# Two sequences taking turns through the attention rounds of a fused attention and FFN block

## The chip, the core and the metric

The kernel runs on one core of a Trainium2 chip. The metric is the device time of one execution in microseconds (us). Lower is better. Five engines work side by side, each through its own list of instructions in the order in which the program issues them: PE (TensorE, matrix products), DVE (VectorE), ACT (ScalarE), POOL (GpSimd) and SP, which does no arithmetic here and starts DMA transfers. An instruction waits at the head of its engine's list for what it needs, and everything behind it on that engine waits too.

## What is computed

The input x holds 4 sequences of 512 positions and 512 features. An attention block whose heads are mixed by a Fourier transform is followed by a gated FFN; both sit on a residual:

```python
x = x + attn(layernorm(x))            # per sequence
#  q, kv = n @ W_q.T, n @ W_kv.T      (16 heads of 32)
#  qf, kvf = fft(q), fft(kv), each head divided by its norm
#  kvf = cumsum(kvf, over positions)
#  attn = ifft(qf * kvf).real @ W_o.T
x = x + ffn(layernorm(x))
#  gate, up, down weights are rounded to fp8 first
#  ffn = down(silu(gate(n) * gate_scale) * up(n) * up_scale) * down_scale
```

All is float32, and the running sum over positions goes through a whole sequence.

## The kernel before

The positions are cut into 16 chunks of 128: 4 sequences (b) of TC = 4 chunks (c). The list `chunks` (L71) holds them sequence by sequence, and a round works on chunk i of this list.

**Prologue (L539 to L614).** The three attention weights come in from SP's queue. Layer norm's centring and the transform are folded into them: `centred` (L203) sums a row block on ACT (L206) and centres it on DVE (L207), `fold_in` (L209) multiplies by the transform. For products of nearly float32 precision a folded weight is then held in three parts: a high part (`split_c`, ACT, L219), a low part (`split_d`, a difference on DVE, L223, and a scaling on POOL, L224), and their difference (`split_e`, L227). Chunk 0 runs through its products in between.

**Rounds (L632 to L682), i = 1 to 15.** A round takes chunk i in, and carries older chunks further:
- PE: `main_part(i)`, 16 matmuls (L266); `cross_part(i)`, 8 (L278); from round 4 on `project(i-4)`, the output product (L397, 4 matmuls shown as 8 records); `running(i-1)`, the running sum as a product with a triangle (L342) of a high part kh and a low part kl.
- ACT: the fp8 rounding of one or two FFN weight units, `rounded` (L143, L144; two units a round until round 5, then one until round 13); `taken(i)` (L289); `k_high(i-1)` (L328); `x_a(i+2)` (L248); `squared(i)` (L296); `rooted(i)` (L306); then, in some rounds, the mean and deviation of a finished chunk of sequence 0 (`y_mean`, `y_deviation`, L423 to L432); last `carry(i-1)`, which copies the end of the running sum (L348) and starts, on ACT's own queue, a small DMA that moves its last row to row 0 (L349).
- DVE: `norms(i-1)` (L311 to L314), `scaled(i-1, 0)` (L319), `products(i-2)` (L357, L358), `finish(i-5)` (L405), `v_turn(i-4)`, a transposition into the one buffer qvT that `project` reads (L377), `summed(i)` (L292), `x_d(i+1)` (L256), in rounds 7 to 10 `y_turn` and its difference (L672), `reduced(i)` (L300).
- POOL: `scaled(i-1, 1)` (L319), `carried(i-1)`, which adds the end row of the chunk before (L324), `combined(i-2)` (L366, L367), `k_low(i-1)` (L333), `x_b(i+2)` (L252).
- SP: loads of inputs and raw weight units (`load_x`, `load_wanted`), the way of a chunk through memory (`v_out`, `v_back`; for sequence 0 also `y_out`, `y_back`), and stores.

The running sum of a chunk needs the end of the chunk before it. In list order that is the previous round: cum(i-1) at the end of round i gives the row that `carried(i)` adds in round i+1.

**The test of the weights (L146 to L199).** In round 14 `flagged` folds sums of the rounded weights into one flag. At the end of round 15's code POOL clears three scratch tiles (L162 to L164), reads the flag and passes a switch; for ordinary weights it jumps over a long arm that would round the weights again. The FFN's products wait for it, since the arm would write the weights.

**FFN (L684 to L769).** For each sequence 12 steps (n counts all 48): 16 matmuls of gate and up (L480), SiLU and product on ACT and DVE, 8 matmuls down (L518). What is left of attention is dealt out to the first steps: `on_pe(0)` the running sum and products of chunk 15, `on_pe(1..4)` the last four `project`, `behind(1..4)` their `finish`. LATE and the tail after L755 set the order of the last steps.

Of the kernel before, what the change touches and what calls it, by code (L numbers as in the profile page):

```python
# [7 lines left out]
F32 = mybir.dt.float32  # L8
# [12 lines left out]
HK = HD // 2  # L21
EPS = 1e-5


# [11 lines left out]
def tile_fft_attention_then_fp8_ffn(  # L36
# [33 lines left out]

    chunks = [(b, c) for b in range(B) for c in range(TC)]  # L71
    N = len(chunks)

    tab = const.tile([P, 3, P], F32, name="tab")
    nc.scalar.dma_start(tab[:, 0, :], tables[:, 0, :])
# [23 lines left out]
    def load_xT(i):  # L101
        xTs[i] = work.tile([P, KC, P], F32, tag="xT", name=f"xT_{i}")
        nc.sync.dma_start(xTs[i], xT[i])

# [51 lines left out]
    def round_again(ok):  # L156
# [7 lines left out]
        on.tensor_copy(f8, a, saturate=False)  # L164
        index = nc.values_load(
# [36 lines left out]

    def centred(raw, j, i):  # L203
        each = work.tile([P, D], BF16, tag="each", name=f"each_w{i}{j}", bufs=1)
        less = small.tile([P, 1], F32, tag="less", name=f"less_w{i}{j}", bufs=8)
        nc.scalar.activation(each, raw[:, j, :], AF.Copy, accum_out=less)  # L206
        nc.vector.tensor_scalar(raw[:, j, :], raw[:, j, :], float(D), less, ALU.mult, ALU.subtract)  # L207

# [112 lines left out]
    def carried(i, on=None):  # L321
        if i in ends:
            row = kqs[i][:1, 0, :]
            (on or nc.gpsimd).tensor_tensor(row, row, ends.pop(i), ALU.add)  # L324

# [19 lines left out]
    def carry(i):  # L345
        if 0 <= i and chunks[i][1] + 1 < TC:
            end = work.tile([P, D], F32, tag="end", name=f"end_{nm(i)}", bufs=1)
            nc.scalar.copy(end[P - 32 :, :], cums[i][P - 32 :, :])  # L348
            nc.scalar.dma_start(end[:1, :], end[P - 1 :, :])  # L349
            ends[i + 1] = end[:1, :]  # L350

# [65 lines left out]
    def y_tile(b, c):  # L417
        return xt[b * TC + c] if b == 0 else ys[b][:, c, :]

    def y_mean(b, c):  # L420
        less = small.tile([P, 1], F32, tag="less", name=f"less_{b}_{c}", bufs=8)
        each = work.tile([P, D], BF16, tag="each", name=f"each_{b}_{c}", bufs=1)
        nc.scalar.activation(each, y_tile(b, c), AF.Identity, accum_out=less)  # L423
        nc.scalar.activation(less, less, AF.Copy, scale=-1.0 / D)
        st_y[b, c] = less

    def y_deviation(b, c):
        less = st_y[b, c]
        rstd = small.tile([P, 1], F32, tag="dev", name=f"dev_{b}_{c}", bufs=8)
        each = work.tile([P, D], BF16, tag="each", name=f"each_d{b}_{c}", bufs=1)  # L430
        nc.scalar.activation(each, y_tile(b, c), AF.Square, bias=less, accum_out=rstd)
        nc.scalar.activation(rstd, rstd, AF.Identity, scale=1.0 / D, bias=eps)  # L432
        nc.gpsimd.tensor_tensor(rstd, rstd, nhalf, ALU.pow)  # L433
        st_y[b, c] = less, rstd

    def y_norm(b, c):
        less, rstd = st_y.pop((b, c))
        xn = work.tile([P, D], F32, tag="xn", name=f"xn_{b}_{c}")
        nc.vector.tensor_scalar(xn, y_tile(b, c), less, rstd, ALU.add, ALU.mult)
        xns["y", b, c] = xn  # L440
        if b == 0:
            del xt[c]

# [108 lines left out]
    for j in range(KC):  # L552
        load_raw(raw_o[j // 2][:, j % 2, :], w_oT, j)
    load_xT(2)
    nc.sync.dma_start(gus[:, 0, :], gate_scale)
# [8 lines left out]
    idle = ps.tile([P, 2, D], F32, tag="tp", name="idle", bufs=1)  # L564
    for n in range(8):
# [6 lines left out]
    for j in range(KC):  # L572
        centred(raw_kv, j, 0)
        for i in range(KC):
            fold_in(pk[i], raw_kv, i, j)
    pq = [ps.tile([P, D], F32, tag="b", name=f"pwq{i}") for i in range(2)]
    t = ps.tile([P, 2, D], F32, tag="tp", name="pwq", bufs=1)
    pq += [t[:, i, :] for i in range(2)]
    for j in range(KC):
        centred(raw_q, j, 1)  # L580
        for i in range(KC):
            fold_in(pq[i], raw_q, i, j)
        if j == 1:
            x_a(0)
            x_b(0)
        split_c(wkv, pk[j], j)
        split_d(wkv, pk[j], j, "kv")
    x_d(0)
    x_a(1)
    x_b(1)  # L590
    main_part(0, 0)
    for i in range(KC):
        split_c(wq, pq[i], i)
        split_d(wq, pq[i], i, "q")
        split_e(wkv, i, nc.vector)
        if i == 1:
            for j in range(2):
                fold_out(raw_o[0][:, j, :], j)
    main_part(0, 1)
    for i in range(KC):  # L600
        split_e(wq, i, (nc.vector, nc.gpsimd)[i % 2])
    taken(0)
    nc.vector.tensor_copy(tri_r, tri)
    cross_part(0)
    x_a(2)
    x_b(2)
    summed(0)
    x_d(1)
    load_xT(3)
    squared(0)  # L610
    reduced(0)
    for j in range(2):
        fold_out(raw_o[1][:, j, :], 2 + j)
    rooted(0)  # L614

# [12 lines left out]
    def load_wanted():  # L628
        while wanted:
            load_unit(wanted.pop(0))  # L630

    for i in range(1, N):  # L632
        at(load_x, i - 4)
        at(v_back, i - 3)
        c = i - 2 - 5
        if 0 <= c < TC:
            y_back(0, c)
# [12 lines left out]
        k_low(i - 1)  # L650
        at(finish, i - 5)
        at(v_turn, i - 4)
        at(x_a, i + 2)
        at(x_b, i + 2)
        at(v_out, i - 2)
        c = i - 1 - 5
        if 0 <= c < TC:
            y_norm(0, c)
            y_out(0, c)
        load_wanted()  # L660
        if i == N - 2:
            ok = flagged()
        if i == N - 1:
            round_again(ok)
        cross_part(i)
        summed(i)
        at(x_d, i + 1)
        at(load_xT, i + 3)
        squared(i)
        c = i - 2 - 5  # L670
        if 0 <= c < TC:
# [7 lines left out]
        if 0 <= c < TC:  # L679
# [11 lines left out]
    scaled(N - 1, 0, nc.vector)  # L691
    scaled(N - 1, 1, nc.gpsimd)
    carried(N - 1)
    combined(N - 2)
    v_back(N - 3)
    load_x(N - 4)
    v_out(N - 2)
    nc.sync.dma_start(dsc, down_scale.partition_broadcast(P))
    k_high(N - 1)
    k_low(N - 1)  # L700
    v_turn(N - 4)
    load_y(0)
    load_x(N - 3)
    v_back(N - 2)
    load_y(1)

    def on_pe(n):
        if n == 0:
            running(N - 1, "tp")
            products(N - 1)  # L710
            combined(N - 1)
            v_out(N - 1)
            v_turn(N - 3)
        elif n <= 4:
            project(N - 5 + n, "tp")

# [5 lines left out]
    def behind(n):  # L722
        b, m = divmod(n, MC)
        if 1 <= n <= 4:
            finish(N - 5 + n)
            if n == 1:
                load_x(N - 2)
                v_back(N - 1)
                v_turn(N - 2)
            elif n == 2:  # L730
                load_x(N - 1)
                v_turn(N - 1)
# [98 lines left out]
```

## Time and profile before

| | us |
|---|---|
| median of 3 runs | 480.39 (479.73 to 483.82) |
| the profiled execution, its time | 482.49 |
| its span, first to last instruction | 480.7 |
| TensorE busy | 445.1, 93% of the span |
| VectorE busy | 242.7, 50% |
| ScalarE busy | 215.7, 45% |
| GpSimd busy | 156.6, 33% |
| mean granted TensorE clock | 0.974 |

The profile page gives busy time per engine, the span in 40 slices, and the costliest groups of instructions. A row of a timeline gives the start, the duration, engine, source line and operation, tile written and tiles read, and in brackets how long the engine was idle before and what ended the idle time. In the text "round r starts at" means the start of its first L266 matmul: 28.8 for round 1, 39.75, 50.35, 60.1, 71.5, 81.4, 95.0, 106.5, 119.35, 130.4, 141.5, 152.6, 162.1, 171.4 and 181.1 for round 15, whose last matmul ends at 190.7.

### The profile page before, as it was taken

What the parts mean: (1) busy time and instruction counts of PE and PEld (TensorE: products, weight loads), DVE (VectorE), ACT (ScalarE), POOL (GpSimd) and SP (SyncE); (2) the same over time, 40 slices, a digit from 0 to 9 for tenths busy, and PEclk for the clock granted to TensorE, in tenths of its full rate; (3) what the DMA queues carried; (4) which work ended last, traced back from release to release, by engine and by line L of the source; (5) the groups of instructions that cost most, each with busy time, mean ns of one, the idle gap of its engine ahead of it and who ended that gap; (6) DMA issues with size and microseconds to landing.
All of it is one profiled execution on the core that took longest, in us unless ns stands there. A gap on an engine that the chain in (4) does not pass through costs nothing.

```text
span 480.7 us, 5386 instructions
## 1 busy us (share of the span) xinstructions
PE 445.1 (93%) x1810; PEld 337.3 (70%) x1810; DVE 242.7 (50%) x373; ACT 215.7 (45%) x386; POOL 156.6 (33%) x153
## 2 busy tenths in 40 slices
PE   8787789888888998599999999999999999999996
PEld 7455556455555665476688888888888888888885
DVE  3866476658888787422433343333352343522235
ACT  6448687767657633211353323543325533222230
POOL 1745765556457756400001231112140022400000
PEclk9998799899999999799999999999999999999999
DMA  8133768577976542493133004141050430100002
GB/s 305 41 109 110 191 173 258 150 201 197 248 204 172 158 109 81 95 262 92 41 89 84 6 35 142 44 105 27 1 175 10 102 65 1 65 24 0 0 1 87
DMA packets 91615, 51.21 MB, mean 107 GB/s; under 512 B 70592, under 2 KB 71104, under 8 KB 91584
## 3 DMA queue, kind: packets, MB, share of 16 engines
q1 hardware_dynamic: 90912, 50.62, 38.1%
q8 instruction: 14, 0.23, 0.2%
q10 hardware_dynamic: 672, 0.22, 0.2%
q14 instruction: 17, 0.14, 0.1%
HBM read 34.03 MB, written 16.78 MB: 106 GB/s over the span
## 4 chain that ended last, share of the span: by engine, by line
PE 57%; issue 1%; POOL 1%; DVE 0%; ACT 0%; POOLq 0%; another core or an unknown queue 0%; DVEq 0%
PE gu L480 36%; PE pd L518 18%; PE po L397 3%; DVE o L529 0%; POOL kl L333 0%; POOL kq L324 0%; POOL kq L319 0%; DVE o L530 0%; PE cum L342 0%; ACT gf L490 0%; ACT kh L328 0%; POOLq L172 0%; POOLq L827 0%; DVEq L529 0%
## 5 line engine op out<-in xcount | busy, mean ns | idle before, releaser
L491 DVE SCALAR_TENSOR_TENSOR gf<-gu,gus,gf 128x512 f32<-128x512 f32 x48 | 35.9, 748 | 124.1 <-PE gu L480 118.3
L480 PE MATMUL gu<-yh,wg 128*128 128x512 f32 x192 | 75.9, 395 | 2.5 <-DVE nt L312 2.5
L518 PE MATMUL pd<-wd,fh 128*128 128x512 f32 (+1 forms) x204 | 77.7, 384 | 0.0
L480 PE MATMUL gu<-yl,wg 128*128 128x512 f32 x192 | 75.8, 395 | 0.0
L518 PE MATMUL pd<-wd,fl 128*128 128x512 f32 (+1 forms) x204 | 75.8, 377 | 0.0
L480 PE MATMUL gu<-yh,wu 128*128 128x512 f32 x192 | 74.7, 389 | 0.0
L480 PE MATMUL gu<-yl,wu 128*128 128x512 f32 x192 | 74.7, 389 | 0.0
L499 ACT CAST fh<-gf 128x512 fp32r<-128x512 f32 x48 | 29.8, 620 | 94.4 <-DVE gf L491 94.4
L397 PE MATMUL po<-wo,qvT 128*128 128x512 f32 x128 | 59.9, 612 | 8.7 <-DVE qvT L377 8.7
L490 ACT ACTIVATE gf<-gu,gus 128x512 f32<-128x512 f32 x48 | 33.1, 689 | 64.6 <-PE gu L480 64.0
L500 DVE TENSOR_TENSOR fl<-gf,fh 128x512 fp32r<-128x512 f32 x48 | 35.9, 747 | 33.1 <-ACT fh L499 33.1
L397 PEld LDWEIGHTS po<-wo,qvT 128*128 128x128 f32 x128 | 24.2, 194 | 36.5 <-issue 28.0
L433 POOL TENSOR_TENSOR dev<-dev,nhalf 128x1 f32<-128x1 f32 x16 | 8.8, 553 | 109.0 <-ACT dev L432 109.0
L518 PEld LDWEIGHTS pd<-wd,fl 128*128 128x128 f32 x204 | 38.4, 188 | 8.1 <-issue 1.0
L518 PEld LDWEIGHTS pd<-wd,fh 128*128 128x128 f32 x204 | 38.3, 188 | 8.2 <-issue 0.7
L480 PEld LDWEIGHTS gu<-yh,wg 128*128 128x128 f32 x192 | 36.7, 191 | 10.3 <-POOLq L172 2.9
L480 PEld LDWEIGHTS gu<-yl,wg 128*128 128x128 f32 x192 | 36.7, 191 | 7.5
L480 PEld LDWEIGHTS gu<-yh,wu 128*128 128x128 f32 x192 | 36.2, 189 | 7.5
L480 PEld LDWEIGHTS gu<-yl,wu 128*128 128x128 f32 x192 | 36.1, 188 | 7.5
L737 POOL TENSOR_TENSOR yl<-t,yh 128x512 fp32r<-128x512 f32 x12 | 15.5, 1293 | 54.9 <-ACT yh L464 54.9
L319 POOL TENSOR_TENSOR kq<-kq,rn 128x512 f32<-128x512 f32 x16 | 21.7, 1355 | 34.9 <-DVE rn L314 28.9
L292 DVE TENSOR_TENSOR kq<-pp,kq 128x1024 f32<-128x1024 f32 x16 | 19.6, 1225 | 21.4 <-PE pp L278 11.8
(109 smaller groups left out, 716.3 us busy)
## 6 DMA issues: line engine op xcount, KB each, us to landing
xT<-in_xT SPq DMA_DIRECT2D x16, 256.0 KB, 4.0
qv_all<-qv SPq DMA_DIRECT2D x16, 256.0 KB, 2.2
zv<-qv_all SPq DMA_DIRECT2D x64, 64.0 KB, 3.7
x<-in_x SPq DMA_DIRECT2D x16, 256.0 KB, 4.4
y_all<-x SPq DMA_DIRECT2D x16, 256.0 KB, 2.1
xn_all<-xn SPq DMA_DIRECT2D x16, 256.0 KB, 2.3
z<-xn_all SPq DMA_DIRECT2D x64, 64.0 KB, 2.6
ys<-y_all SPq DMA_DIRECT2D x16, 256.0 KB, 4.0
```

The costliest lines, as they stand in the source:

```text
L292: nc.vector.tensor_tensor(kqs[i], sqs.pop(i), kqs[i], ALU.add)
L319: on.tensor_tensor(t, t, r, ALU.mult)
L397: nc.tensor.matmul(po, lhsT=qvT[:, k, :], rhs=wo[:, k, :], start=k == 0, stop=k == KC - 1)
L433: nc.gpsimd.tensor_tensor(rstd, rstd, nhalf, ALU.pow)
L480: nc.tensor.matmul(p, lhsT=w[:, k, m * P : (m + 1) * P], rhs=v[:, k, :], start=k == 0 and v is yhs[b], stop=k == KC - 1 and v is yls[b],)
L490: nc.scalar.activation(g, pgu[0], AF.Silu, scale=gus[:, 0, m : m + 1])
L491: nc.vector.scalar_tensor_tensor(f, pgu[1], gus[:, 1, m : m + 1], g, ALU.mult, ALU.mult)
L499: nc.scalar.copy(fh, f)
L500: nc.vector.tensor_tensor(fl, f, fh.bitcast(F32), ALU.subtract)
L518: nc.tensor.matmul(p, lhsT=v[:, c * P : (c + 1) * P], rhs=wd[:, m, s], start=m == 0 and v is fused[n][0], stop=m == MC - 1 and v is fused[ ...
L737: nc.gpsimd.tensor_tensor(*y_turn(b + 1, m - 7), ALU.subtract)
```

## The change

- The list of chunks alternates between two sequences: (0,0), (1,0), (0,1), (1,1) and so on, then sequences 2 and 3. The end of a chunk is now needed two list places later.
- The end row's DMA goes from ACT's queue to SP's, at the head of the next round (`carry_on`).
- Order inside a round. ACT: `rooted(i-1)` and `carry(i-2)` stand at the head of round i, so `rooted` comes after the mean and deviation. DVE: `reduced` ahead of `y_turn`. POOL: `x_b(i+1)` at the head, `carried` ahead of `scaled(.., 1)`, and the difference of `y_turn`, which leaves DVE. SP: `carry_on`, `v_back`, `y_back`, `load_x`, units. Sequence 0 is finished in rounds 5, 7, 9, 11 (mean and deviation), turned in 7, 9, 11, 13.
- The low part of a folded weight is one DVE operation that reads PSUM; two of the row sums of W_q go to DVE, its centring to POOL.
- The switch is moved up in round 15, ahead of `combined(13)` and `k_low(14)`, and the three clears are gone.
- The last running sum, the four last `project` and `finish` come one FFN step later, and `scaled(15, 1)` on POOL comes after `k_low(15)`.

The diff, cut to its core:

```diff
-    chunks = [(b, c) for b in range(B) for c in range(TC)]
+    chunks = [(b + d, c) for b in range(0, B, 2) for c in range(TC) for d in range(2)]
+    place = {bc: i for i, bc in enumerate(chunks)}
...
-        on.memset(ab, 0.0)
-        on.memset(cd, 0.0)
-        on.tensor_copy(f8, a, saturate=False)
...
     def split_c(w, pw, i):
-        nc.scalar.activation(w[0][:, i, :], pw, AF.Copy, scale=UNDER)
+        nc.scalar.activation(w[0][:, i, :], pw, AF.Copy, scale=UNDER / SPLIT)
-    def split_d(w, pw, i, name):
-        d = work.tile([P, D], F32, tag="cross", name=f"d_{name}{i}")
-        nc.vector.tensor_tensor(d, pw, w[0][:, i, :].bitcast(F32), ALU.subtract)
-        nc.gpsimd.tensor_scalar(w[1][:, i, :], d, SPLIT, 1.0, ALU.mult, ALU.mult)
+    def split_d(w, pw, i):
+        nc.vector.scalar_tensor_tensor(
+            w[1][:, i, :], w[0][:, i, :].bitcast(F32), -SPLIT, pw, ALU.mult, ALU.add
+        )
...
     def carry(i):
-        if 0 <= i and chunks[i][1] + 1 < TC:
-            end = work.tile([P, D], F32, tag="end", name=f"end_{nm(i)}", bufs=1)
+        b, c = chunks[i]
+        if c + 1 < TC:
+            end = work.tile([P, D], F32, tag="end", name=f"end_{nm(i)}")
             nc.scalar.copy(end[P - 32 :, :], cums[i][P - 32 :, :])
-            nc.scalar.dma_start(end[:1, :], end[P - 1 :, :])
-            ends[i + 1] = end[:1, :]
+            ends[i] = end
+    def carry_on(i):
+        if i in ends:
+            end = ends.pop(i)
+            nc.sync.dma_start(end[:1, :], end[P - 1 :, :])
+            b, c = chunks[i]
+            ends[place[b, c + 1], "row"] = end[:1, :]
...
-    for j in range(KC):
-        centred(raw_q, j, 1)
+    def fold_q(j, on_act):
+        centred(raw_q, j, row_sum(raw_q, j, 1, on_act), nc.gpsimd)
         for i in range(KC):
             fold_in(pq[i], raw_q, i, j)
...
     for i in range(1, N):
+        rooted(i - 1)
+        at(carry, i - 2)
+        at(carry_on, i - 2)
+        at(v_back, i - 3)
+        if (c := y_due(i, 2)) is not None:
+            y_back(0, c)
         at(load_x, i - 4)
-        at(v_back, i - 3)
...
         load_wanted()
         norms(i - 1)
         scaled(i - 1, 0, nc.vector)
+        at(x_b, i + 1)
+        carried(i - 1)
         scaled(i - 1, 1, nc.gpsimd)
         at(products, i - 2)
-        carried(i - 1)
+        if i == N - 2:
+            ok = flagged()
+        if i == N - 1:
+            round_again(ok)
         at(combined, i - 2)
...
         squared(i)
-        c = i - 2 - 5
-        if 0 <= c < TC:
-            nc.vector.tensor_tensor(*y_turn(0, c), ALU.subtract)
         reduced(i)
+        if (c := y_due(i, 2)) is not None:
+            nc.gpsimd.tensor_tensor(*y_turn(0, c), ALU.subtract)
+        rounded(i, 1)
+        if (c := y_due(i, 0)) is not None:
+            y_mean(0, c)
+            y_deviation(0, c)
         at(project, i - 4)
         running(i - 1)
-        rounded(i, 1)
-        rooted(i)
-        c = i - 5
-        if 0 <= c < TC:
-            y_mean(0, c)
-            y_deviation(0, c)
-        carry(i - 1)
...
     def on_pe(n):
-        if n == 0:
+        if n == 1:
             running(N - 1, "tp")
...
-        elif n <= 4:
-            project(N - 5 + n, "tp")
+        elif 2 <= n <= 5:
+            project(N - 6 + n, "tp")
```

`y_due(i, late)` gives the chunk of sequence 0 that is due, in every second round: `c, odd = divmod(i - late - 5, 2)`.

More of the change, by code (lines that the diff above doesn't have):

```diff
@@ L199, in round_again, with row_sum, centred @@
                     on.tensor_copy(to[:, k, :], c)
-    def centred(raw, j, i):
-        each = work.tile([P, D], BF16, tag="each", name=f"each_w{i}{j}", bufs=1)
+    def row_sum(raw, j, i, on_act=True):
         less = small.tile([P, 1], F32, tag="less", name=f"less_w{i}{j}", bufs=8)
-        nc.scalar.activation(each, raw[:, j, :], AF.Copy, accum_out=less)
-        nc.vector.tensor_scalar(raw[:, j, :], raw[:, j, :], float(D), less, ALU.mult, ALU.subtract)
+        if on_act:
+            each = work.tile([P, D], BF16, tag="t8", name=f"each_w{i}{j}", bufs=1)
+            nc.scalar.activation(each, raw[:, j, :], AF.Copy, scale=-1.0, accum_out=less)
+        else:
+            nc.vector.tensor_reduce(less, raw[:, j, :], AX.X, ALU.add, negate=True)
+        return less
+    def centred(raw, j, less, on):
+        on.tensor_scalar(raw[:, j, :], raw[:, j, :], float(D), less, ALU.mult, ALU.add)
     def fold_in(pw, r, i, j):
@@ L321, in carried @@
     def carried(i, on=None):
-        if i in ends:
+        if (i, "row") in ends:
             row = kqs[i][:1, 0, :]
-            (on or nc.gpsimd).tensor_tensor(row, row, ends.pop(i), ALU.add)
+            (on or nc.gpsimd).tensor_tensor(row, row, ends.pop((i, "row")), ALU.add)
     def k_high(i):
@@ L417, in y_tile @@
     def y_tile(b, c):
[L418 removed]
+        return xt[place[b, c]] if b == 0 else ys[b][:, c, :]
     def y_mean(b, c):
         less = small.tile([P, 1], F32, tag="less", name=f"less_{b}_{c}", bufs=8)
[L422 removed]
+        each = work.tile([P, D], BF16, tag="t8", name=f"each_{b}_{c}", bufs=1)
         nc.scalar.activation(each, y_tile(b, c), AF.Identity, accum_out=less)
@@ L441, in y_norm @@
         if b == 0:
-            del xt[c]
+            del xt[place[b, c]]
     def y_out(b, c):
@@ L564, in tile_fft_attention_then_fp8_ffn @@
     idle = ps.tile([P, 2, D], F32, tag="tp", name="idle", bufs=1)
-    for n in range(8):
+    for n in range(10):
         nc.tensor.matmul(
@@ L578, in tile_fft_attention_then_fp8_ffn @@
     pq += [t[:, i, :] for i in range(2)]
-    for j in range(KC):
-        centred(raw_q, j, 1)
+    def fold_q(j, on_act):
+        centred(raw_q, j, row_sum(raw_q, j, 1, on_act), nc.gpsimd)
         for i in range(KC):
             fold_in(pq[i], raw_q, i, j)
[L583 to L587, printed above, removed]
+    fold_q(0, True)
+    split_c(wkv, pk[0], 0)
+    fold_q(1, False)
+    split_d(wkv, pk[0], 0)
+    x_a(0)
+    x_b(0)
+    for i in range(1, KC):
+        split_c(wkv, pk[i], i)
+        split_d(wkv, pk[i], i)
+        if i == 1:
+            fold_q(2, True)
+    fold_q(3, False)
+    main_part(0, 0)
+    x_a(1)
+    for i in range(2):
+        split_e(wkv, i, nc.gpsimd)
     x_d(0)
-    x_a(1)
-    x_b(1)
-    main_part(0, 0)
     for i in range(KC):
         split_c(wq, pq[i], i)
-        split_d(wq, pq[i], i, "q")
-        split_e(wkv, i, nc.vector)
+        split_d(wq, pq[i], i)
         if i == 1:
@@ L598, in tile_fft_attention_then_fp8_ffn @@
                 fold_out(raw_o[0][:, j, :], j)
+    split_e(wq, 0, nc.gpsimd)
+    for i in range(2, KC):
+        split_e(wkv, i, nc.vector)
     main_part(0, 1)
-    for i in range(KC):
-        split_e(wq, i, (nc.vector, nc.gpsimd)[i % 2])
+    split_e(wq, 1, nc.gpsimd)
+    for i in range(2, KC):
+        split_e(wq, i, nc.vector)
     taken(0)
-    nc.vector.tensor_copy(tri_r, tri)
+    x_b(1)
+    load_xT(2)
     cross_part(0)
     x_a(2)
-    x_b(2)
     summed(0)
+    squared(0)
     x_d(1)
     load_xT(3)
-    squared(0)
+    nc.vector.tensor_copy(tri_r, tri)
     reduced(0)
@@ L630, in load_wanted, with y_due @@
             load_unit(wanted.pop(0))
+    def y_due(i, late):
+        c, odd = divmod(i - late - 5, 2)
+        return c if not odd and 0 <= c < TC else None
     for i in range(1, N):
+        rooted(i - 1)
[4 more added lines that the diff above has]
+            y_back(0, c)
         at(load_x, i - 4)
-        at(v_back, i - 3)
-        c = i - 2 - 5
-        if 0 <= c < TC:
-            y_back(0, c)
         load_wanted()
@@ L652, in tile_fft_attention_then_fp8_ffn @@
         at(v_turn, i - 4)
[L653 to L656, printed above, removed]
-        if 0 <= c < TC:
+        if (c := y_due(i, 1)) is not None:
             y_norm(0, c)
```

41 lines of the change are left out of this document (18 added, 23 removed).

## The prediction

> **What bounds the kernel now.** I read the page first, then busy time by stretch, then each engine's timeline in the rounds, and last the waits.
>
> ```profile
> PE 445.1 (93%) x1810; PEld 337.3 (70%) x1810; DVE 242.7 (50%) x373; ACT 215.7 (45%) x386; POOL 156.6 (33%) x153
> PEclk9998799899999999799999999999999999999999
> ```
>
> TensorE is busy for 93%, but that is an average. The stretches are rounds 1-3, 4-5, 6-7, 8-12, 13-15, the change-over to the FFN, and the rest (PE, PEld, DVE, ACT, POOL busy; then clock):
>
> ```profile
> 28.80:60.10 31.30, 23.93 (x81) 17.69 (x80) 17.33 (x30) 22.88 (x35) 17.32 (x15) 0.84 0.54 157
> 60.10:81.40 21.30, 19.50 (x69) 12.54 (x68) 15.80 (x24) 16.49 (x25) 12.53 (x12) 1.00 0.74 197
> 81.40:106.50 25.10, 21.25 (x69) 13.07 (x68) 16.07 (x28) 18.02 (x33) 14.60 (x15) 0.93 0.69 192
> 106.50:162.10 55.60, 49.93 (x172) 32.65 (x171) 46.17 (x71) 36.16 (x62) 34.63 (x32) 0.97 0.74 195
> 162.10:190.70 28.60, 28.55 (x105) 19.03 (x103) 22.53 (x39) 12.34 (x20) 18.90 (x19) 1.00 0.44 119
> 190.70:207.90 17.20, 10.60 (x34) 7.92 (x35) 6.43 (x13) 4.67 (x7) 6.61 (x8) 0.80 0.48 138
> 207.90:475.00 267.10, 267.10 (x1169) 216.54 (x1168) 97.44 (x141) 90.20 (x177) 37.26 (x36) 1.00 0.22 59
> ```
>
> From 207.9 on TensorE never pauses, so nothing there can be won. Rounds 13-15 are full too: 9.4 us each is TensorE's own work in a round. All that can move lies ahead of 162 and in the change-over. What stops TensorE there:
>
> ```profile
> 106.17 0.50 PE L342 MATMUL cum<-kl,tri_r 128*128 128x512 f32 x1 [1.81 <-POOL kl L333]
> ...
> 108.13 0.63 PE L266 MATMUL pa<-wkv,xb 128*128 128x512 f32 x1
> ...
> 148.64 3.67 PE L397 MATMUL po<-wo,qvT 128*128 128x512 f32 x8 [1.53 <-DVE qvT L377]
> ```
> ```profile
> 83.43 0.21 ACT L306 ACTIVATE rn<-ss 128x32 f32<-128x32 f32 x1
> 83.55 0.62 ACT L423 ACTIVATE each<-x 128x512 bf16<-128x512 f32 x1
> ...
> 85.69 0.58 ACT L348 COPY end<-cum 32x512 f32<-32x512 f32 x1
> ```
> ```profile
> 90.27 1.26 POOL L324 TENSOR_TENSOR kq<-kq,end 1x512 f32<-1x512 f32 x1 [2.94 <-DMA end<-end]
> ...
> 190.44 0.61 POOL L164 CAST again<-again_ab 128x512 fp8e4<-128x512 f32 x1
> 197.05 1.05 POOL L319 TENSOR_TENSOR kq<-kq,rn 128x512 f32<-128x512 f32 x1 [5.99 <-issue]
> ```
>
> The projection (L397) waits for the transposed chunk, which comes late because DVE's round is late. The end copy (L348) stands behind 2.1 us of mean and deviation, so in rounds 6 to 8 POOL waits for the end row. At the switch POOL is empty for 6.0 us. A matmul costs 0.23 us from start to start, but 0.43 after some gaps (108.13): the clock is halved there.
>
> **The change, part by part.**
>
> *Prologue, -2.7.* Eight POOL scalings (3.6 + 3.3 us, L224) and their hops go; waits on them show as 2.1 us of TensorE idle (L266). DVE's form still takes one pass, 0.69 us by L223. Against that, the fourth block of W_q is centred on POOL behind x_b: 0.8 to 1.0 us by L224 in place of 0.49, so fold-in ends about 1 us later. From there: ACT splits W_q with no wait for POOL, DVE's last `split_e` ends about 24.3 (four passes of 0.6 after the last low part at 21.9, while POOL does four others in 15.5 to 20.9), the cross product ends 24.6 instead of 27.5, two fold-outs take 1.3. Round 1 starts at 26.1, not 28.8. Bounds: -1.4 (POOL ops at their contended 1.65 us, L227) to -3.5.
>
> *Rounds 1-3, -0.9.* Round 1 still waits for the first raw unit, which lands 4.05 us after its issue. ACT sheds a DMA issue of 0.5 to 0.6 us a round (L349). In round 2 chunk 1 has no end row to wait for, so kl comes 1.4 earlier and the half-clock stretch at 50.4 (13 matmuls, 0.2 each) falls away. In round 3 kl waits behind `carried`, `scaled` and `combined` on POOL (1.3 + 1.5 + 1.4), so 2.7 us idle and a slow clock come one round later. Bounds -3.0 to +1.0.
>
> *Rounds 4-5, +2.4.* Here SP's order costs. `carry_on` waits for ACT's end copy, which follows `rooted` by 0.6 us; behind it stand four `v_back` (2.6 us to issue) and a load of x, then the raw unit that `rounded(i,1)` needs in the same round, landing 4.2 us after issue. By ACT's order that unit is wanted at about `rooted` + 6.0 (end copy 0.6, a unit 2.2, L289 1.0, L328 and L248 1.1, L296 1.0), and it lands at 0.6 + 0.5 + 2.6 + 0.5 + 4.2 = 8.4: ACT stalls about 2.4 us in rounds 3, 4 and 5. TensorE has 1.0 us of slack (projection ready 4.35 us after `rooted` ends, needed 5.48 after the round starts, `rooted` normally ending 0.1 after it). Round 4 starts at 56.5, round 6 at 80.2: 23.7 for 21.3. Bounds: 0 less 2.0 (units in time) to +5.
>
> *Rounds 6-7, -1.3.* Round 6 starts with the unit's stall and 2.1 us of mean and deviation ahead of `rooted`: projection at 88.9 as before (88.95), same slow clock, 14.4 us for 13.6. Round 7 then runs at 9.4 instead of 11.5, since no end row is awaited. Bounds -3.5 to +1.5.
>
> *Rounds 8-12, +2.4.* Odd rounds 7, 9, 11 now have on ACT, ahead of `rooted`, the copy of the turned chunk (which waits for `reduced` and the transposition) and the 2.1 us of mean and deviation. From `summed`: 2.32 to `reduced`, 1.14 its turn, 0.73 transposition, 0.52 copy, 2.14, 0.23: 7.1 us instead of 3.8. Of the 3.3 later, 1.0 is slack: rounds 8, 10 and 12 wait 2.3 us for the projection (2.9 in 8 and 12, where the reload of z is issued behind `carry_on` and `v_back`). Lengths 12.0, 9.4, 11.7, 9.4, 12.3 = 54.8 against 55.6. So the old waits of 1.0 to 1.9 in each round become 2.3 to 2.9 in every second. After waits of 1.8 and 1.9 us the clock was halved (1.6 us lost on average over 89.0, 107.3 and 202.6), after 2.47 at 193.1 it was not; I take two of three: +3.2. Moving the difference to POOL adds 1.3 us (L737) where POOL has 2 to 4 us free ahead of `carried`. Bounds -0.8 to +6.
>
> The skill page TensorE: Matmul & The Clock Gate, section "Why this matters for your kernels", says drops need idle gaps over about 3 us; this trace shows them after 1.81 and 1.90. By the page no round here would slow, and this term would be -0.8.
>
> *Rounds 13-15, +4.4.* Round 14 gets 0.8 from the last turning ahead of `rooted(13)`. In round 15 POOL reaches the switch at about 4.0 (`scaled0` 1.5, `carried` 1.3, `scaled1` 1.2), is empty for 6.0 until 10.0, then `combined` 1.4 and `k_low` 1.3: kl at 12.7, where TensorE wants it at 8.9. Behind the switch also wait products(14) and so the whole chain of chunk 15. Round 15 takes 13.4 instead of 9.5. The hole lies between 2.1 us (193.13, where the FFN's first product was let go, less 191.05) and 6.0; I take 6.0, since the next POOL instruction is what counts. Bounds 0 to +5.
>
> The page Runtime: NRT & Kernel Launch, "Instruction fetch mechanics", calls a taken branch out of the fetch window a stall for a fetch from memory; it gives no length.
>
> *Change-over, -7.4.* It takes 17.2 now: 2.5 until the switch lets go, 3.6 of products, 2.95 + 1.22 waiting for kh and kl of chunk 15, sums, 3.6 + 1.6 at the slow clock. After: products at once, 3.6 + 1.6 (slow clock behind round 15's gap), 0.4 for SiLU queued behind kh, 3.6, then the running sum 0.5, kl ready about 2 us earlier: 9.8. The four projections, a step later, cost what they cost (3.43 each). Bounds -9 to -4.
>
> FFN: the same work. Later `finish` leaves y of sequence 1 loaded in step 1 and read in step 3, over 9 us later, where a load lands in 4.0: 0. Fewer clears (2.5 us on POOL) lie beside other work: 0.
>
> **Sum.** -2.7 - 0.9 + 2.4 - 1.3 + 2.4 + 4.4 - 7.4 = -3.1. On the profiled execution 482.49 gives 479.4; that execution lay 2.1 above the median, so against 480.4 I say 477.3.
>
> **Rivals.**
> *Units in time and a steady clock.* If raw units land before ACT wants them (in rounds 1 to 3 they had up to 8 us), rounds 4-5 give -2.0 instead of +2.4, and without slow clock in 8-12 the term is -0.8: -3.1 - 4.4 - 3.2 = -10.7, 469.7. For: transfers took 74% of the DMA engines, not all. Against: the wait of 2.7 us that ACT already had on a raw unit in round 5, with an earlier issue.
>
> *The clock, slower.* Fewer and longer waits are worse if each halves the clock. It decides at the length that triggers it: at 1.8 us or less, rounds 4, 5, 8, 10 and 12 all slow, for up to 2.5 us each (the 13 matmuls at 50.4). Against my sum that adds 1.7 (rest of round 4) + 1.6 (round 5) + 7.5 - 3.2 (three at 2.5) and 0.8 in round 6: +8.4, so +5.3: 485.7. For: 1.81 and 1.90. Against: 2.47 at 193.1, and 1.53 at 148.6.
>
> *The reload of z is late.* In round 7 before it landed 2.4 us after DVE wanted it. If so in rounds 7, 11 and 13 beyond my 0.6, 3 x 1.9 = +5.7: 483.
>
> **How the numbers follow.** Chances: my sum 0.45 (its own range 474 to 481), units in time 0.27, the clock 0.18, z 0.10. Faster by over 1% (about what a measurement here can tell from no change) means below 475.6: all of the second case and 0.13 of the first: 0.40. Slower, above 485.2: most of the third, and tails of the first and fourth: 0.24. Within: 0.36. The range from 468 to 487 holds the second case's centre and the third's and leaves about a fifth out.
>
> **What would show it.** Right: round 1 starts near 26; in rounds 8, 10, 12 the projection waits over 2 us for qvT, hardly in 9 and 11; in round 15 the running sum waits about 4 us for kl, with POOL empty 6 us ahead of `combined`; no wait for chunk 15's kh in the FFN. Wrong: ACT idle on raw units under 1 us in rounds 3 to 5, a hole at the switch under 3 us, or a pause of TensorE in the FFN after the first six steps.

## The result, and the profile after

The changed kernel takes 494.63 us (median of 4 runs, 492.91 to 494.82) beside 480.42 for the kernel before (4 runs): a ratio of 1.027 (95% interval 1.022 to 1.033). I had said 477.3, within 468 to 487: a gain, where the change is a loss. The profiled execution took 492.91 us, its span is 491.1, 10.4 longer than before.

From the page of the changed kernel (line numbers are those of the kernel profiled, so L411 here is what L397 was before): TensorE has the same work and is busy 3 us longer, and the clock row has six eights and a seven in its first seventeen slices, where it had two of each.

```profile
PE 448.0 (91%) x1814; PEld 339.8 (69%) x1814; DVE 240.5 (49%) x365; ACT 214.8 (44%) x382; POOL 151.7 (31%) x152
PEclk9898899798999898999999999999999999999999
```

Busy time by stretch of the changed kernel, for the same stages as the prediction's table (rounds 1-3, 4-5, 6-7, 8-12, 13-15, the change-over, the rest; PE, PEld, DVE, ACT, POOL, clock, DMA share, GB/s):

```profile
29.50:59.90 30.40, 21.44 (x80) 15.93 (x79) 20.33 (x32) 23.62 (x35) 15.80 (x14) 0.89 0.51 149
59.90:83.05 23.15, 20.68 (x70) 14.00 (x69) 13.82 (x23) 16.35 (x24) 12.46 (x12) 0.92 0.61 169
83.05:109.40 26.35, 20.63 (x69) 13.36 (x68) 16.51 (x25) 16.42 (x27) 13.32 (x13) 0.87 0.61 179
109.40:173.80 64.40, 53.78 (x171) 33.99 (x170) 45.53 (x71) 36.78 (x65) 37.16 (x35) 0.89 0.66 181
173.80:208.25 34.45, 30.72 (x106) 19.58 (x104) 24.04 (x36) 13.85 (x21) 17.23 (x17) 0.95 0.41 101
208.25:218.30 10.05, 8.14 (x35) 6.41 (x35) 5.81 (x11) 3.62 (x6) 4.89 (x5) 1.00 0.69 151
218.30:485.40 267.10, 267.10 (x1169) 216.52 (x1168) 98.75 (x143) 90.19 (x177) 38.59 (x38) 1.00 0.23 62
```

The last row has the same 1169 matmuls in the same 267.10 us as before, so all of the loss lies ahead of it. The fourth row holds most: 64.40 us instead of 55.60, of which TensorE idles 10.6 (5.7 before), at a clock of 0.89 (0.97 before). Every second round is long. Round 10 shows how; first TensorE, then ACT, VectorE and GpSimd, all of the changed kernel:

```profile
144.31 5.37 PE L411 MATMUL po<-wo,qvT 128*128 128x512 f32 x8 [3.25 <-DVE qvT L391]
```
```profile
136.21 0.62 ACT L478 CAST yh<-t 128x512 fp32r<-128x512 f32 x1 [2.09 <-DVE t L391]
...
138.77 0.21 ACT L313 ACTIVATE rn<-ss 128x32 f32<-128x32 f32 x1
```
```profile
134.15 1.22 DVE L307 TENSOR_REDUCE ss<-sq 128x32 f32<-128x1024 f32 x1 [0.50 <-ACT sq L303]
135.46 0.71 DVE L391 STREAM_TRANSPOSE t<-z 128x512 f32<-128x512 f32 x1
139.01 0.35 DVE L318 RECIPROCAL rn<-rn 128x32 f32<-128x32 f32 x1 [2.84 <-ACT rn L313]
...
139.63 1.17 DVE L320 SCALAR_TENSOR_TENSOR nt<-nt,ss 128x32 f32<-128x32 f32 x1
...
143.47 0.70 DVE L391 STREAM_TRANSPOSE qvT<-zv 128x512 f32<-128x512 f32 x1
```
```profile
139.45 1.30 POOL L259 TENSOR_TENSOR xb<-xT,xa 128x512 fp32r<-128x512 f32 x1
```

Read from the bottom up: the projection waits 3.25 us for qvT, which VectorE writes late in its round. VectorE had idled 2.84 us for the root (`rn`), which stands on ACT behind the turned copy, mean and deviation. That is what I had forecast, as a wait of 2.3. The other 0.98 us is one small operation, `nt` of L320, which takes 1.17 us instead of 0.19: it begins 0.18 us after GpSimd's `x_b`, which the change put at the head of the round, and ends with it. It takes 1.16 to 1.21 us in rounds 6, 8, 10, 12 and 14 of the changed kernel, each time beside `x_b`, and 0.19 in every other round. In round 8 VectorE waits a further 1.11 us for the reload of z, and the projection 4.17 us. After such a wait a projection takes 4.8 to 6.0 us up to the running sum instead of 3.0 to 3.1: the granted clock over it is 0.64 in round 10 and 0.51 in round 8, where over the projection of round 9, which did not wait, it is 1.00.

### The profile page after: what moved, and what is told of

Same layout as the page of the kernel before. It is cut to its first block, busy times and chain, and to the rows that moved or that the text cites. A ratio compares the mean times of both kernels' runs of the same rounds, so it can differ in the third digit from the quotient of the medians.

```text
span 491.1 us, 5365 instructions
## 1 busy us (share of the span) xinstructions
PE 448.0 (91%) x1814; PEld 339.8 (69%) x1814; DVE 240.5 (49%) x365; ACT 214.8 (44%) x382; POOL 151.7 (31%) x152
## 4 chain that ended last, share of the span: by engine, by line
PE 65%; DMA 9%; DVE 7%; ACT 7%; SPq 6%; issue 4%; POOL 2%; DVEq 0%; POOLq 0%; ACTq 0%
PE gu L494 35%; PE pd L532 18%; PE po L411 6%; SPq L386 5%; DMA z<-xn_all 3%; DMA qv_all<-qv 3%; PE pa L273 2%; DMA rawf<-in_gate_w 2%; PE pp L285 1%; DMA rawf<-in_up_w 1%; PE idle L579 1%; ACT t L147 1%; DVE nt L320 1%; DVE kq L299 1%; ACT end L356 1%
## 5 line engine op out<-in xcount | busy, mean ns | idle before, releaser
L411 PE MATMUL po<-wo,qvT 128*128 128x512 f32 x128 | 67.6, 678 | 22.3 <-DVE qvT L391 13.4
L494 PE MATMUL gu<-yl,wg 128*128 128x512 f32 x192 | 74.8, 390 | 0.0
L513 ACT CAST fh<-gf 128x512 fp32r<-128x512 f32 x48 | 29.8, 621 | 82.0 <-DVE gf L505 82.0
L504 ACT ACTIVATE gf<-gu,gus 128x512 f32<-128x512 f32 x48 | 33.1, 689 | 74.1 <-PE gu L494 73.8
L411 PEld LDWEIGHTS po<-wo,qvT 128*128 128x128 f32 x128 | 27.2, 217 | 54.1 <-issue 32.5
L514 DVE TENSOR_TENSOR fl<-gf,fh 128x512 fp32r<-128x512 f32 x48 | 36.6, 763 | 33.1 <-ACT fh L513 32.3
L273 PE MATMUL pa<-wkv,xa 128*128 128x512 f32 x64 | 28.0, 438 | 0.0
```

What stands on the lines that cost most here:

```text
L273: nc.tensor.matmul(pas[i][:, j, :], lhsT=v[:, k, :], rhs=u[:, k, :], start=k == 0 and u is w[0], stop=k == KC - 1 and u is w[1],)
L411: nc.tensor.matmul(po, lhsT=qvT[:, k, :], rhs=wo[:, k, :], start=k == 0, stop=k == KC - 1)
L494: nc.tensor.matmul(p, lhsT=w[:, k, m * P : (m + 1) * P], rhs=v[:, k, :], start=k == 0 and v is yhs[b], stop=k == KC - 1 and v is yls[b],)
L504: nc.scalar.activation(g, pgu[0], AF.Silu, scale=gus[:, 0, m : m + 1])
L513: nc.scalar.copy(fh, f)
L514: nc.vector.tensor_tensor(fl, f, fh.bitcast(F32), ALU.subtract)
```

## Experiments

All times are medians; the ratio is to runs of the kernel before on the same chip. The stages of the profiled executions, in us, by the round starts in the timelines (the last column is the span less 272.8, the time from the end of the change-over on in the kernel before and in the changed one, less the start of the FFN's products; for the kernel before and for before + turns the cut lies at the end of round 15's last matmul, after which the FFN's first product waits another 2.5 and 1.7 us):

| kernel | time | ratio (95%) | prologue | 1-3 | 4-7 | 8-12 | 13-15 | change-over |
|---|---|---|---|---|---|---|---|---|
| before | 480.4 | 1 | 28.8 | 31.3 | 46.4 | 55.6 | 28.6 | 17.2 |
| changed | 494.6 | 1.027 (1.022-1.033) | 29.5 | 30.4 | 49.5 | 64.4 | 34.4 | 10.1 |
| root early | 489.5 | 1.022 (1.017-1.028) | 29.9 | 30.5 | 46.6 | 62.6 | 33.1 | 9.9 |
| SP's order | 486.3 | 1.013 (1.007-1.019) | 31.6 | 31.2 | 42.6 | 61.7 | 33.6 | 11.6 |
| root early, SP's order | 470.7 | 0.985 (0.979-0.990) | 29.7 | 30.6 | 40.7 | 51.3 | 33.7 | 10.1 |
| root early, store ahead | 480.6 | 1.002 (0.999-1.006) | 31.6 | 30.5 | 46.0 | 55.7 | 34.5 | 10.2 |
| root early, end row behind | 482.9 | 1.007 (1.003-1.010) | 30.2 | 30.9 | 40.9 | 63.2 | 33.0 | 10.0 |
| prologue's move | 489.1 | 1.018 (1.013-1.022) | 26.7 | 31.9 | 49.4 | 63.0 | 33.8 | 10.0 |
| filler, second form | 491.7 | 1.026 (1.020-1.032) | 30.8 | 31.1 | 49.3 | 61.3 | 34.7 | 11.7 |
| before + turns | 476.8 | 0.993 (0.990-0.997) | 28.3 | 30.5 | 40.8 | 55.6 | 29.5 | 17.0 |
| before + last stages, switch up | 477.2 | 0.997 (0.994-1.000) | 27.9 | 29.8 | 46.3 | 54.4 | 32.9 | 10.8 |
| before + turns + last stages | 470.5 | 0.983 (0.978-0.988) | 27.7 | 30.3 | 40.8 | 57.7 | 30.3 | 9.7 |
| all mended | 464.6 | 0.968 (0.965-0.971) | 26.4 | 31.4 | 41.1 | 51.6 | 29.5 | 10.5 |

My theory after the result: ACT's order ahead of the root makes the projection late, and each wait halves TensorE's clock for a while. The rivals: SP's queue brings the reload late; taking turns is itself the loss; the clock alone.

**The root back in its own round.**

```diff
     for i in range(1, N):
-        rooted(i - 1)
         at(carry, i - 2)
...
         reduced(i)
+        rounded(i, 1)
+        rooted(i)
         if (c := y_due(i, 2)) is not None:
             nc.gpsimd.tensor_tensor(*y_turn(0, c), ALU.subtract)
-        rounded(i, 1)
```

> The changed kernel (494.6 us) with only the root taken back into its own round, ahead of the copy of the turned chunk and of the mean and deviation. Theory (ACT's order ahead of the root makes the projection late, and each wait halves the clock): the root of rounds 7, 9, 11 and 13 comes 2.8 us earlier, so the waits of 3.2 to 4.2 us ahead of the projections of rounds 8, 10, 12 and 14 fall below 1.3 us, and with them the slow projections (5.4 to 6.6 us, back to 3.6); round 15 then gives up to 3 us back at the switch: 477 to 484 us. Rival, the transposed chunk is late because SP's queue brings it late: the waits stay over 2 us, 490 to 494. Rival, the clock drops after any gap: waits short, projections still at 5.4 us, about 487.

489.5 us, not the expected 477 to 484: the waits of rounds 8, 10, 12 and 14 are 3.81, 4.48, 2.26 and 2.10 us. My theory failed as it stood. VectorE's timeline of this kernel shows what took the root's place:

```profile
129.77 1.23 DVE L307 TENSOR_REDUCE ss<-sq 128x32 f32<-128x1024 f32 x1 [0.50 <-ACT sq L303]
134.48 0.71 DVE L391 STREAM_TRANSPOSE t<-z 128x512 f32<-128x512 f32 x1 [3.48 <-DMA z<-xn_all]
```

The root is done at 131.3, but the transposition of the turned chunk stands ahead of the norms on VectorE and waits 3.48 us for its reload. In all, VectorE waits 8.5 us for z here; in the changed kernel it was 1.8, since the rounds were so long that z had mostly landed. SP's own timeline of this kernel says why z is late:

```profile
120.29 0.44 SPq L142 DMA_DIRECT2D rawf<-in_up_w  x1
120.82 0.75 SPq L394 DMA_DIRECT2D qv_all<-qv  x1
...
127.04 2.60 SPq L386 DMA_DIRECT2D zv<-qv_all  x4
129.68 2.67 SPq L386 DMA_DIRECT2D z<-xn_all  x4
```

The reloads of qv (`zv`) wait for its store, which the change put behind a load of 512 KB; they go out 6.2 us after its issue, and the reload of the turned chunk (`z`) stands behind them.

**SP's order.**

```diff
-        at(carry_on, i - 2)
         at(v_back, i - 3)
         if (c := y_due(i, 2)) is not None:
             y_back(0, c)
+        load_wanted()
+        at(carry_on, i - 2)
         at(load_x, i - 4)
-        load_wanted()
...
+        at(v_out, i - 2)
         load_wanted()
-        at(v_out, i - 2)
```

> The changed kernel with only SP's order altered: the store of qv ahead of the load of a raw unit in mid round, and at the head of a round the transposing reloads and the raw unit ahead of the move of the end row, which waits for ACT's end copy. Theory (ACT's order): in rounds 9, 11 and 13 the reload is there when VectorE gets to it, so nothing is won after round 8; ACT's waits for raw units in rounds 3 to 5 (2.6, 2.7 and 3.5 us) and the late start of round 7 shrink: 490 to 494. Rival, SP's order is what makes the projections late: their waits fall by 2 us or more each and the clock recovers, 478 to 486.

486.3 us, between what the theory (490 to 494) and its rival (478 to 486) had said. Rounds 4 to 7 take 42.6 instead of 49.5, rounds 8 to 12 only 2.7 less: with the root still behind, the projections wait 2.99, 3.07 and 3.08 us and are slow.

**Both together.**

> The changed kernel with both edits together: the root in its own round ahead of the turned copy, mean and deviation, and SP's order altered (store of qv ahead of a raw unit; reloads ahead of the move of the end row). Alone they gave 5 and 8 us. Theory now: two lines, ACT's order and SP's reload of the turned chunk, both end at the projection of rounds 8, 10, 12 and 14, and whichever is left still makes it wait; with both gone VectorE finds the reload there and the root done, the waits fall below 1.3 us and rounds 8 to 12 take under 53 us instead of 64.4: 474 to 480 us. Rival, the two edits free the same slack and something else (VectorE beside GpSimd, the end copy) holds the projection: 483 to 487.

470.7 us, better than the expected 474 to 480. By the medians the edits alone had given 5 and 8 us, and together they give 24 (by the ratios 2, 7 and 20; the first of these lies within the intervals). The kernel now beats the one before. Rounds 6-7 and 8-12 by stretch, with the clock at 1.00:

```profile
80.90:101.05 20.15, 19.20 (x70) 12.65 (x68) 16.07 (x27) 14.89 (x27) 13.43 (x13) 1.00 0.79 204
101.05:152.34 51.29, 48.03 (x171) 31.62 (x170) 44.96 (x66) 36.73 (x64) 36.41 (x35) 1.00 0.77 213
```

The waits of rounds 8, 10 and 12 are 0, 0.91 and 0.91 us. Two lines ended at the same wait, and removing one left the other. `nt` takes 0.19 us in every round here, as it does with the root early alone, though `x_b` stands at the head of the round as before: with the root early the two no longer meet.

**Which half of SP's order.** The same kernel with only the store moved (the second hunk above), and with only the first hunk: the end row's move behind the reloads and the raw unit, and the raw unit ahead of the load of x.

> The changed kernel with the root in its own round, and of the two edits of SP's order only one: the store of qv goes out ahead of the raw unit. Both together gave 470.7 us. Theory: what makes the reloads late is that the store, issued behind a load of 512 KB, lands 6.2 us after its issue (3.5 when it is ahead), and the transposing reloads wait for it; so this edit carries nearly all: 470 to 474 us. Rival, it is the move of the end row, which waits for ACT's end copy at the head of SP's round: 482 to 489.

> The changed kernel with the root in its own round, and of the two edits of SP's order only the other one: the reloads and the raw unit ahead of the move of the end row; the store of qv stays behind the raw unit. Theory (the store behind 512 KB): little is won over the root's move alone (489.5), 483 to 489 us, VectorE still waits for the turned chunk's reload in rounds 9 to 13. Rival, the end row's wait is what holds SP: 470 to 475.

480.6 us, where I had said 470 to 474, and 482.9, at the edge of 483 to 489: the store doesn't carry nearly all of it, as I had thought. The table tells the halves apart by stage, beside the root early alone: the end row's move acts in rounds 4 to 7 (40.9 instead of 46.6), the store in rounds 8 to 12 (55.7 instead of 62.6; with both 51.3). SP's waits for the end copy, with the root early alone and with the end row behind as well:

```profile
SPq L362 <- ACT end L356: 40.6, 12, 6.6
```
```profile
SPq L362 <- ACT end L356: 1.5, 1, 1.5
```

(Total, times, longest.) While SP waited there, the raw unit that ACT wanted stood behind: ACT's waits for raw units are 10.1 us with the root early alone, 2.9 with the end row behind. For the store, its line of the DMA issues (times, size, median us to landing), with the root early alone and with both halves:

```profile
qv_all<-qv SPq DMA_DIRECT2D x16, 256.0 KB, 5.0
```
```profile
qv_all<-qv SPq DMA_DIRECT2D x16, 256.0 KB, 2.3
```

With one half it is 3.5 (store ahead) and 4.0 (end row behind), so both shorten it. In the kernel before it had been 2.2, in the changed one 4.3.

**Turns alone.** The kernel before with the alternating list, the end row kept two places, and sequence 0 due in every second round. To make room for a second end row, the tables and a scratch tile share buffers with others; nothing else differs.

```diff
-    chunks = [(b, c) for b in range(B) for c in range(TC)]
+    chunks = [(b + d, c) for b in range(0, B, 2) for c in range(TC) for d in range(2)]
...
-            ends[i + 1] = end[:1, :]
+            ends[place[b, c + 1]] = end[:1, :]
...
-        c = i - 5
-        if 0 <= c < TC:
+        if (c := y_due(i, 0)) is not None:
             y_mean(0, c)
```

> The kernel before (480.4 us) with only the two sequences taking turns: the end row is needed a round later, sequence 0 is finished in rounds 5, 7, 9 and 11. ACT's order, POOL's order, the prologue, the switch and the last stages stay as before (to make room for a second end row, the tables and a scratch tile share buffers). Theory: taking turns is no loss by itself; the waits for the end row in rounds 2 and 6 to 8 go (1.4 us in round 2, some 3 us in rounds 6 to 8) and the waits of the projection in rounds 8 to 12 stay as they were or shrink: 473 to 479. Rival, taking turns is itself what loses (two chunks' chains meet in one round): 484 to 492.

476.8 us, as the theory had it, and the interval of the ratio (0.990 to 0.997) leaves 1 out. Rounds 6 and 7 fall from 25.1 to 19.6 us, rounds 8 to 12 stay at 55.6. Taking turns is a gain, a small one; it was the orders around it that lost.

**The clock, filled.** Extra matmuls ahead of the late projections. The first form wrote into the projection's own tile and settled nothing:

> The changed kernel with 13 extra matmuls (3.0 us at full clock) into the projection's own PSUM tile just ahead of the projections of rounds 8, 10, 12 and 14; their sums are overwritten by the projection. TensorE then idles for 0.2 to 1.2 us instead of 3.2 to 4.2, while the transposed chunk comes no earlier. Theory: the slow projections (6.60 and three times 5.37 us instead of 3.6) are the clock's answer to the idle time, so they go back to 3.6: minus 7 to 8 us, 486 to 489. Rival, the clock follows something else (a schedule or the load), or what it loses is hidden: 493 to 496.

494.7 us (ratio 1.0315, 1.0255 to 1.0375). That tile's buffer comes free only when VectorE has read the sum of chunk i-2 from it, so TensorE now waited for that (1.77, 2.80 and 1.85 us) and ran the filler afterwards. The second form:

```diff
         cross_part(i)
+        if i in (8, 10, 12, 14):
+            filler(i, 13)
         summed(i)
```

> The changed kernel with 13 extra matmuls (3.0 us at full clock) in rounds 8, 10, 12 and 14, now into a PSUM tile that is free at that time, issued behind the cross product, so that TensorE can run them while it would wait for the transposed chunk; their result is not used. Theory: the slow projections (6.60 and three times 5.37 us) are the clock's answer to the idle time ahead of them and go back to 3.6 us, while the time at which each projection can start stays: 486 to 489 us beside 494.6. Rival, the clock does not follow the idle time, or what it loses is hidden: 493 to 496.

491.7 us, not told apart from the changed kernel, where I had said 486 to 489. Rounds 8, 12 and 14 have short waits (0 to 0.87 us), fast projections, and take 12.6, 13.4 and 13.1 us instead of 16.7, 14.5 and 14.9. But round 10 takes 16.6 instead of 14.5: its round came earlier while z did not, and VectorE waits 2.17 us for it; round 15 gives 2.0 back behind the switch. So the clock's loss follows the idle time, as expected, but what the filler saves is mostly lost again to lines that don't run by TensorE's time.

**The prologue.**

```diff
     for i in range(KC):
         split_c(wq, pq[i], i)
         split_d(wq, pq[i], i)
-        if i == 1:
-            for j in range(2):
-                fold_out(raw_o[0][:, j, :], j)
+    for j in range(2):
+        fold_out(raw_o[0][:, j, :], j)
```

> The changed kernel with one move in the prologue: the first two fold-outs of W_o, and ACT's copies of them, behind the four splits of W_q instead of between the second and the third. Theory: those copies wait for TensorE's products of chunk 0 and hold the splits of the third and fourth block by 2.5 us; without them round 1 starts at 27 to 28.5 us instead of 29.5 to 31.6, which is carried to the end: 491 to 493.5 us where the changed kernel takes 494.6. Rival, the centring of W_q on GpSimd or the raw weights' arrival sets the start: it stays at 29.3 or later, no gain.

Round 1 starts at 26.7, and 489.1 us is 4.6 less by the ratios, more than expected. ACT in the changed kernel, then in this one:

```profile
16.75 1.08 ACT L226 ACTIVATE wq<-pwq 128x512 fp32r<-128x512 f32 x2 [2.84 <-PE pwq L217]
21.36 0.59 ACT L241 COPY wo<-pwo 128x512 f32<-128x512 f32 x1 [3.52 <-PE pwo L240]
...
22.70 0.60 ACT L226 ACTIVATE wq<-pwq 128x512 fp32r<-128x512 f32 x1
```
```profile
16.43 1.08 ACT L226 ACTIVATE wq<-pwq 128x512 fp32r<-128x512 f32 x2 [2.84 <-PE pwq L217]
17.71 0.60 ACT L226 ACTIVATE wq<-pwq 128x512 fp32r<-128x512 f32 x1 [0.20 <-PE pwq L217]
```

**The last stages and the switch.** The kernel before with only the last stages a step later, the clears gone and the switch up:

> The kernel before with only the end of the change: the last running sum, projections and finishes one FFN step later, the clears gone and the switch moved up in round 15 ahead of combined and k_low. Theory: the change-over gives 7 us as in the changed kernel, but here TensorE is in time in rounds 14 and 15, so GpSimd's hole behind the switch (4.7 to 6.0 us) shows: GpSimd gets to the switch at the start of the round plus 4.9 us, kl of chunk 14 is ready at plus 12.3 to 13.6 where the running sum wants it at plus 9.1, so 3.1 to 4.4 us come back: 476 to 478 us. Rival, the hole is hidden as in the changed kernel (0.28 us): 473.

477.2 us. TensorE and GpSimd of this kernel at the end of round 15:

```profile
186.19 0.80 PE L339 MATMUL cum<-kh,tri_r 128*128 128x512 f32 x1
190.89 0.50 PE L339 MATMUL cum<-kl,tri_r 128*128 128x512 f32 x1 [3.90 <-POOL kl L330]
```
```profile
180.74 1.29 POOL L321 TENSOR_TENSOR kq<-kq,end 1x512 f32<-1x512 f32 x1 [0.20 <-DMA end<-end]
188.14 0.70 POOL L363 TENSOR_TENSOR qv<-qv 128x240 f32<-128x240 f32 x1 [6.11 <-DVE x L402]
```

The hole of 6.11 us behind the switch costs 3.90, within the expected 3.1 to 4.4; VectorE had done the products that GpSimd works on next at 180.8. In the changed kernel TensorE comes late itself, and the hole costs nearly nothing:

```profile
205.12 0.70 POOL L380 TENSOR_TENSOR qv<-qv 128x240 f32<-128x240 f32 x1 [4.73 <-issue]
```
```profile
207.88 0.51 PE L349 MATMUL cum<-kl,tri_r 128*128 128x512 f32 x1 [0.28 <-POOL kl L340]
```

With the turns, and the switch left at the end of the round:

> The kernel before with the two sequences taking turns (476.8 us by itself) and the last stages one FFN step later, the clears gone, but the switch left at the end of round 15. Theory: the last stages give their 7 us on top, and the switch costs nothing there, since without the clears GpSimd gets to it about 2.5 us earlier and lets the FFN go before TensorE gets there: 468 to 471 us. Rival, the hole behind the switch now holds carried, combined and k_low of the last chunks, which TensorE wants one step into the FFN: 472 to 475.

470.5 us, as expected: a gain of 6 us on the turns alone (5 by the ratios).

**All mended.** The changed kernel with the root early, SP's order, the prologue's move, and the flag and the switch at their old places:

```diff
-        if i == N - 2:
-            ok = flagged()
-        if i == N - 1:
-            round_again(ok)
         at(combined, i - 2)
...
         at(x_a, i + 2)
+        if i == N - 2:
+            ok = flagged()
+        if i == N - 1:
+            round_again(ok)
         cross_part(i)
```

> The changed kernel with the root in its own round, both edits of SP's order, the prologue's move, and the flag and the switch back at their places of the kernel before (mid round 14 and the end of round 15, still without the clears). Theory: beside 470.7 us, the prologue's 1.5 to 2 us, and 2 to 3.5 us in rounds 14 and 15 (2.1 us of waiting with a slow clock behind the flag's VectorE work, 1 us behind the hole): 465 to 468 us. Rival, the hole behind the switch then holds chunk 15 in the FFN and the prologue's start does not move: 469 to 472.

464.6 us, just under the expected 465 to 468 and 3.2% (2.9 to 3.5) faster than the kernel before. It is also 6 us faster than turns and last stages without the change's other parts, so these parts gain too once their orders are right. Rounds 13 to 15 take 29.5 us instead of 33.7 and the prologue 26.4; TensorE's waits for the projections add up to 2.8 us, where the changed kernel had 22.3.

## Why the prediction was wrong, point by point

In spans my sum was -3.1, the measured one +10.4.

- **Prologue, -2.7: failed, +0.7.** The work was nearly as I counted: round 1 starts at 26.7 where I said 26.1, once ACT's order lets it. I wrote that ACT splits W_q with no wait for POOL; two copies of W_o stood in its list between the second and third split, as in the kernel before (at 18.48 and 19.33 there), and now waited for TensorE until 21.36. I priced the operations and not the queue.
- **Rounds 1-3, -0.9: right,** -0.9, with the wait of round 3 for kh and kl at 2.00 and 2.39 us.
- **Rounds 4-5, +2.4: right** in mechanism, +1.9. ACT waited 2.58, 2.72 and 3.48 us for raw units where I said 2.4, and with the end row's move behind the reloads the loss goes.
- **Rounds 6-7, -1.3: failed, +1.3.** Round 7 took the 9.4 us I gave it, but round 6 17.0 instead of 14.4: the late units and the root behind mean and deviation held it, its projection waited 5.72.
- **Rounds 8-12, +2.4: this is the step that failed, +8.8.** The place and the mechanism were right: rounds 8, 10 and 12 wait, 9 and 11 do not and take 9.4. The lengths were 16.7, 14.5 and 14.5, not 12.0, 11.7 and 12.3. TensorE's three waits add up to 10.6 us where these lengths had 7.8, and the slow clock behind them to 6.5 where I had 3.2. In round 10 the wait is my 2.3 plus 1.0 for `nt` beside GpSimd's `x_b`, which I had put at nothing; round 12 is alike, and in round 8 the reload of z adds up to 1.1, where I had allowed 0.6. The 1.0 is read from the rows: no run takes it away by itself. I had costed the new place of work on GpSimd by GpSimd's free time, not by what VectorE does beside it. And I never priced SP's mid-round order: the store of qv behind the raw unit, which makes the reload the next thing to be late as soon as the root is not.
- **The clock.** I took two of three waits to be slow, at 1.6 us each. All three were, for 3.0 us in round 8 and 1.8 in rounds 10 and 12; each wait had grown past 3 us. Over the profiled executions of all these kernels but the first filler, of the projections between 60 and 200 us of the span: 115 with a wait up to 1.65 us, none slow; 20 with 1.81 to 2.84 us, 10 slow; 19 with 2.99 us or more, all slow. A slow one takes 4.8 us in most cases (4.5 to 6.0) instead of 3.1. The Trainium skill's page TensorE: Matmul & The Clock Gate, section "Why this matters for your kernels", advises no idle gaps over about 3 us. The measurement agrees above that and differs below: between 1.8 and 2.9 us the drop comes in half of the cases.
- **Rounds 13-15, +4.4: a sum that was nearly right (+5.9) from wrong parts.** Round 14 took 14.9 us: its root stood behind the last turning, its projection waited 3.46 us and ran slowly. I had given it 0.8. So TensorE was late in round 15, and a hole of 4.73 us at the switch cost 0.28, where I had taken some 3.8. With TensorE in time, as with the last stages alone, a hole of 6.11 costs 3.90.
- **Change-over, -7.4: right,** -7.1, with no wait for kh or kl of chunk 15; the second product waited 1.91 us for SiLU, without the slow clock I had added. These 1.91 happen to equal the 0.4 for SiLU and 1.6 for the clock in my sum, so how closely the term fits is in part luck.
- **The rivals.** "The clock, slower" (485.7) and "the reload of z late" (483) each had a part of the truth. I had set them beside my sum as alternatives with chances of their own. They add up in one and the same wait: about 2.3 of order, 1.0 of contention and up to 1.1 of reload pass the length at which the clock drops, and then 1.8 to 3.0 more follow.
- **The signs of being wrong.** None of the three I had named came: ACT waited 2.58 to 3.48 us for raw units, the hole was 4.73, and TensorE did not pause in the FFN after 218.3. They guarded the terms I had priced, not those I had left out.

## What to carry to other kernels

Waits that end at the same instruction are not rivals: list every line that ends there, with its time of arrival, since taking one away shows only the next, and two edits that give little alone (here 5 and 8 us) may give much together (24). When a change reorders several queues, price the DMA queue line by line, above all a store that others wait for and that now goes out behind a large load, and whatever stands behind an instruction that waits. A good idea (taking turns, 0.993 by itself) can hide in a bundle that is slower.

## What the runs showed of the hardware

- A small VectorE operation beside a GpSimd one was not slowed in proportion but held to its end: in the changed kernel and in the one with SP's order alone, `nt` took 1.16 to 1.21 us instead of 0.19 in ten of ten such rounds and ended within 0.1 us of `x_b`. The Trainium skill's page SBUF — State Buffer, section "SBUF: two separate sides", describes an exclusive lock between VectorE operations with two inputs there and GpSimd operations that read there; these rows agree with it.
- GpSimd stood empty for 4.73 us behind the switch in the changed kernel and for 6.11 with the last stages alone, as for 5.99 in the kernel before. What fills these holes no run here shows.
- The same prologue code had round 1 start between 29.5 and 31.6 in eight profiled executions, so a gain of 1 us there can't be read from one execution.
- What remains open: why the prologue's move gained 4.6 us in time where round 1 came 2.8 us earlier. The intervals of the two ratios are wide enough to hold both, and so is the chance of slow projections between 1.8 and 2.9 us of waiting; no run here settles it.
